# Two transformer layers with routed experts on one core: deeper row buffers and a pinned scaling in the last stage of layer 1

## The chip, the cores and the metric

The kernel runs on one core of a Trainium2 chip. The metric is the device time of one execution in microseconds (us), taken as the median of several runs. A core has five engines that work side by side, each through its own queue of instructions in order: TensorE (PE in the profile; its weight loads are PEld), VectorE (DVE), ScalarE (ACT), GpSimd (POOL) and SyncE (SP). [...] Transfers go out from the queues of SP (loads and stores) and of POOL (gathers by index) to 16 DMA engines that all of them share.

## The reference

The input is a residual stream x of 4 sequences of 512 rows with 512 features, 2048 rows in all. Each of the two layers computes

    xn = layernorm(x)
    x  = x + attention(xn) + experts(xn)

Layer 0 has a sparse and local attention with 16 heads of 128 and eight experts, of which each row takes two. Layer 1, where the change is, has a plain softmax attention with 16 heads of 32, and this feed-forward part:

    logits = xn @ router_w;  the best two of 8 experts, gates = softmax of the two
    combined = gate0 * silu(xn @ W[e0]) + gate1 * silu(xn @ W[e1])
    y = xn + combined @ proj_w + proj_b
    result = norm_w * y / sqrt(mean(y*y) + 1e-6)

Everything is float32. The last stage of the kernel, called the mixing here, is the lower three lines of this block, mixed with the last groups of layer 1's attention.

## The kernel before, in words

**Tiles.** The 2048 rows are 16 tiles of 128 rows (`n` = 0 to 15). The experts have written their results to a table `yd` in memory, one row for each pair of row and expert. The attention runs over 16 groups `g` (sequence `b`, four heads `j`), each with four steps `kc` of 128 keys: scores `st` (L1322), their exponentials `pT` on ACT (L1324), the context `cx` (L1336), and on DVE the running sum `pS` of the exponentials (L1342, two instructions a step from `kc` = 1 on). Beside them run the queries and keys of the next group (`qp`, L1298, finished on DVE in L1303 to L1313), once per group the sum over keys (`sm`, L1350) with reciprocals (L1360) and the scaled context (L1368), for the last sequence its values by seven products (`vp`, L1258, finished on DVE in L1262 to L1272), and for each tile of rows the attention's output product (`o`, L1405).

**Who sets the order.** A list `jobs1` puts each step of the experts and of the mixing at a place (g, kc). For tile n the mixing has four steps at four places one behind the other:

    for d, f in ((0, mix), (1, turn_mix), (2, project_mix), (3, finish_mix)):
        jobs1.append((at[here + d], lambda n=n, f=f: f(n)))

with `here` moving on by 13 places for 16 tiles. `mix` issues two gathers on POOL for the two expert rows of each token (`row0`, `row1`, L545), a load of xn (`xa`, L1435), the two gate scalings on DVE (L1438 and L1439), and adds the bias on POOL (L1440). `turn_mix` transposes the sum on PE (`trc`, L1447) and copies it out on ACT (`combT`, L1451). `project_mix` multiplies by proj_w on PE (`po`, L1458), adds the product to xa on DVE (L1459), squares on ACT (L1462) and forms the inverse root on POOL (`yss`, L1463 and L1464). `finish_mix` scales on DVE (L1469) and adds the result to the residual row.

**The order on an engine.** Within these places the order of instructions on each engine is chosen when the program is built, by the framework's scheduler; `tc.keep_in_program_order` keeps an instruction where the program has it. In `mix` the first scaling of tiles 0 and 1 is kept so (`pin`), that of the later tiles is not.

**Residual rows.** The two parts of a row's result, attention (`way` 0) and mixing (`way` 1), arrive at different times. `bring` (L1390) loads the old residual row from memory (`accd`) into a free place, `add_part` (L1394) adds a part on DVE and then stores the row, to `out` (L1397) where both parts are in, and back to `accd` (L1399) where one is still to come. If the row lies already in one place for the other part, nothing is loaded.

**Banks.** The products `vp`, `qp`, `trc`, `po`, `o` and `sm` take turns in three PSUM banks (`bank1("mm", ...)`). PE can begin the product after the next two only when the reader of the first, on DVE or ACT, is done. The DVE instructions that free a bank are L1264 to L1272, L1303 to L1313, L1394 (for `o`) and L1459; ACT frees those of `trc` and `sm`.

**Buffers.** In the mixing's pool each name has two buffers if nothing else is said. The gathered rows have one buffer each, so POOL gathers tile n+1's `row0` when PE has transposed tile n's, and its `row1` when DVE has used tile n's.

Of the kernel before, what the change touches and what calls it, by code (L numbers as in the profile page):

```python
# [12 lines left out]
F32 = mybir.dt.float32  # L13
I32 = mybir.dt.int32
AF = mybir.ActivationFunctionType
ALU = mybir.AluOpType
# [4 lines left out]
P = 128  # L21
B, S, HID = 4, 512, 512
# [3 lines left out]
KC = HID // P  # L26
# [23 lines left out]
def two_layers(ctx: ExitStack, tc: tile.TileContext, a: dict, out: bass.AP, large: bass.AP):  # L50
# [4 lines left out]
    V, G, A, PE = nc.vector, nc.gpsimd, nc.scalar, nc.tensor  # L55
# [20 lines left out]
    def load(pool, name, shape, src):  # L76
        t = pool.tile(shape, F32, tag=name, name=name, bufs=1)
        nc.sync.dma_start(out=t, in_=src)
        return t
# [376 lines left out]
    def at_rows(idx):  # L456
        return bass.IndirectOffsetOnAxis(ap=idx, axis=0)

    class Experts:
# [80 lines left out]
        def gather(self, n):  # L540

            rs = []
            for k in range(2):
                x = self.pool.tile([P, HID], F32, tag=f"row{k}", name=f"row{k}_{self.r.name}_{n}")
                G.indirect_dma_start(out=x, out_offset=None, in_=self.yd,  # L545
                                     in_offset=at_rows(self.r.slot[:, k, n : n + 1]))
                rs.append(x)
            return rs
# [87 lines left out]
    rout = {}  # L636
# [544 lines left out]
    rows = {"wv_b": load(w1p, "wv_b", [P, HID], a["wv_b"].partition_broadcast(P))}  # L1181
# [3 lines left out]
    NJ = NH1 * D1 // P  # L1185
# [88 lines left out]
    def queries(g, i):  # L1274
        b, j = groups1[g]
        if i == 0:
            qk[g] = ap_.tile([P, 2, S], F32, tag="qk", name=f"qk_{g}")
        if b:
            return queries7(g, i)
        qp_ = bank1("mm", f"qp_{g}_{i}")  # L1280
        for k in range(KC):
            PE.matmul(qp_, lhsT=wa[("wqT", "wkT")[i]][:, k, ts(j, P)], rhs=xnT[:, k, ts(b, S)],
                      start=(k == 0), stop=(k == KC - 1))
        V.tensor_scalar(qk[g][:, i, :], qp_, qkb[:, i, j : j + 1], None, ALU.add)
# [30 lines left out]
    def weights(g, kc):  # L1315

        pt = ap_.tile([P, HJ, S], F32, tag="pT", name=f"pT_{g}_{kc}")
        for pair in range(HJ // 2):
            st = psum1("st", f"st_{g}_{kc}_{pair}", 2)
            for i in range(2):  # L1320
                rows_ = ds((2 * pair + i) * D1, D1)
                tc.keep_in_program_order(PE.matmul(st[:, i, :], lhsT=qk[g][rows_, 1, ts(kc, P)], rhs=qk[g][rows_, 0, :],  # L1322
                                                   start=True, stop=True))
            A.activation(pt[:, ts(pair, 2), :], st, AF.Exp, scale=SCALE1)  # L1324
        return pt
# [3 lines left out]
    def attend(g, kc, pt):  # L1329
        b, j = groups1[g]  # L1330
        if kc == 0:
            acc_cx[g] = psum1("cx", f"cx1_{g}")[:, 0, :]
            acc_pt[g] = ap_.tile([P, HJ, S], F32, tag="pS", name=f"pS_{g}", bufs=1)
            first_pt[g] = pt
        for h in range(HJ):
            tc.keep_in_program_order(PE.matmul(acc_cx[g][ds(h * D1, D1), :], lhsT=v[b][:, kc, ds(j * P + h * D1, D1)], rhs=pt[:, h, :],  # L1336
                                               start=(kc == 0), stop=(kc == TC - 1)))

        if kc > 0:
            before = first_pt.pop(g) if kc == 1 else acc_pt[g]  # L1340
            for pair in range(HJ // 2):
                V.tensor_tensor(acc_pt[g][:, ts(pair, 2), :], before[:, ts(pair, 2), :], pt[:, ts(pair, 2), :], ALU.add)  # L1342
# [3 lines left out]
    def sum_keys(g):  # L1346

        sm = bank1("mm", f"sm1_{g}")
        for h in range(HJ):
            PE.matmul(sm[ds(h * D1, D1), :], lhsT=ones, rhs=acc_pt[g][:, h, :], start=True, stop=True)  # L1350
        del acc_pt[g]
        cs = ap_.tile([P, S], F32, tag="cs", name=f"cs_{g}", bufs=1)
        A.copy(cs, acc_cx.pop(g))
        rs = ap_.tile([P, S], F32, tag="rsum", name=f"rsum_{g}", bufs=1)
        A.activation(rs, sm, AF.Copy, accum_out=ends[:, 1, g : g + 1])
        parts[g] = cs, rs

    def invert(g, t):
        rs = parts[g][1]
        V.reciprocal(rs[:, ts(t, P)], rs[:, ts(t, P)])  # L1360
# [12 lines left out]
    def scale_context(g):  # L1373
        scale_chunk(g)
        largest_sum(g)
# [4 lines left out]
    def bring(n, way):  # L1380

        if (n, 1 - way) in lies:
            lies[n, way] = lies[n, 1 - way]
            return
        if n < NT - TC:

            lies[n, way] = acc[:, 3 * TC + n % TC, :] if way else xnT[:, 3 if n + 1 < NT - TC else 0, 0:S]
        elif left[n] == 2:
            lies[n, 0] = lies[n, 1] = acc[:, n, :]
        nc.sync.dma_start(out=lies[n, way], in_=accd[ts(n, P), :])  # L1390

    def add_part(n, part_, way):
        x = lies.pop((n, way))
        V.tensor_tensor(x, x, part_, ALU.add)  # L1394
        left[n] -= 1
        if left[n] == 0:
            nc.sync.dma_start(out=out_v[n], in_=x)  # L1397
        elif (n, 1 - way) not in lies:
            nc.sync.dma_start(out=accd[ts(n, P), :], in_=x)  # L1399

    def output1(b, t):
        n = b * TC + t
        op = bank1("mm", f"o1_{n}")
        for jj in range(NJ):
            PE.matmul(op, lhsT=cT1[b][:, jj, ts(t, P)], rhs=wa["woT"][:, jj, :],  # L1405
                      start=(jj == 0), stop=(jj == NJ - 1))
        add_part(n, op, 0)
# [23 lines left out]
    def mix(n):  # L1431

        g0, g1 = rout["ex1"].gather(n)
        x = rout["mix"].tile([P, HID], F32, tag="xr", name=f"xa_{n}")
        nc.sync.dma_start(out=x, in_=xnd[ts(n, P), :])  # L1435

        pin = tc.keep_in_program_order if n < 2 else (lambda x: x)
        pin(V.tensor_scalar(g0, g0, r1.gate[:, 0, n : n + 1], None, ALU.mult))  # L1438
        V.scalar_tensor_tensor(g0, g1, r1.gate[:, 1, n : n + 1], g0, ALU.mult, ALU.add)  # L1439
        G.tensor_tensor(x, x, rows["pb"], ALU.add)  # L1440
        held[n] = g0, x

    def turn_mix(n):
        g0, x = held[n]
        tr = bank1("mm", f"trc_{n}")
        for f in range(KC):
            PE.transpose(tr[:, ts(f, P)], g0[:, ts(f, P)], ident)  # L1447
        bring(n, 1)
        cT_ = rout["mix"].tile([P, KC, P], F32, tag="xT", name=f"combT_{n}")

        A.activation(cT_, tr.rearrange("p (k t) -> p k t", k=KC), AF.Copy, scale=0.5)  # L1451
        held[n] = cT_, x
# [13 lines left out]

    def finish_mix(n):
        y, ss = held.pop(n)
        V.scalar_tensor_tensor(y, y, ss[:, 0:1], rows["nw1"], ALU.mult, ALU.mult)  # L1469
        add_part(n, y, 1)  # L1470


# [30 lines left out]
    for n in range(NT):  # L1503
        here = first + n * 13 // 16
        for d, f in ((0, mix), (1, turn_mix), (2, project_mix), (3, finish_mix)):
            jobs1.append((at[here + d], lambda n=n, f=f: f(n)))
# [30 lines left out]
    for g in range(NG):  # L1537
        b, j = groups1[g]
        for kc in range(TC):
            nxt = weights(g, kc)  # L1540
            if late is not None:
                attend(*late)
            late = (g, kc, nxt)
            if g > 0:
                if kc == 1:
                    sum_keys(g - 1)
                    invert(g - 1, 0)
                if kc == 2:
                    invert(g - 1, 1)
                    invert(g - 1, 2)  # L1550
                if kc == 3:
                    invert(g - 1, 3)
                    scale_context(g - 1)
            if kc < 2 and g + 1 < NG:
                queries(g + 1, kc)
            if kc > 1 and j + 1 == NJ and 1 < b + 1 < B:
                values7(b + 1, kc - 2)

            if kc == 1 and g > NJ:
                bring(g - NJ - 1, 0)  # L1560
            if kc == 2 and g + 1 == NG:
                bring(NT - TC - 1, 0)
            if kc == 3 and g > NJ:
                output1(*divmod(g - NJ - 1, TC))
            run1((g, kc))
# [716 lines left out]
```

## Time and profile before

| | us |
|---|---|
| median of 3 runs | 2043.84 |
| lowest, highest | 2041.92, 2044.12 |
| the profiled execution | 2039.16 |
| its span, first to last instruction | 2037.1 |
| outside the span | 2.1 |
| PE busy in the span | 1983.6 (97%) |
| DVE busy | 1506.5 (74%) |
| ACT busy | 868.5 (43%) |
| POOL busy | 746.3 (37%) |
| mean granted TensorE clock | 0.995 |

The span is counted from the first instruction; all places in time below are us from there. The mixing begins at about 1845 us, when the last product of the experts is done, and its last scaling runs at about 2008 us. Behind it the last outputs of the attention end the span. Times of groups of instructions are given with their line, the engine, the operation and the tiles written and read. "[1.12 <-DVE xnT L1394]" behind a row of the timeline says that the engine stood idle for 1.12 us ahead of it, and that an L1394 instruction on DVE ended the wait.

### The profile page before, as it was taken

The page shows a single profiled execution, that of the slowest core. Times are in us where ns is not written, and L with a number is a line of the kernel's source. Part 1 is how long each engine was busy: PE and PEld are TensorE (multiplying, and loading weights), DVE is VectorE, ACT ScalarE, POOL GpSimd, SP SyncE. Part 2 cuts the span into 40 slices and gives each one's busy share as a digit, 9 for nine tenths or more (in the row PEclk, how much of TensorE's full clock was granted, in tenths as well). Part 3 has the DMA queues.
Part 4 walks back from the last instruction along what each step waited for, and adds up shares of the span by engine and source line. Part 5 has one row for each costly group of instructions (what it writes and reads, how often), then busy time and mean ns, then how long its engine had stood idle before and what let it go on. Part 6 is the DMA issues. An engine that isn't in the chain of part 4 may idle for free.

```text
span 2037.1 us, 28573 instructions
## 1 busy us (share of the span) xinstructions
PE 1983.6 (97%) x9358; PEld 1243.6 (61%) x9358; DVE 1506.5 (74%) x3696; ACT 868.5 (43%) x2600; POOL 746.3 (37%) x761
## 2 busy tenths in 40 slices
PE   7999999999999999999999999999999999999998
PEld 4666667777777777767667666666334445445443
DVE  7889968777776777786678878788596555557775
ACT  4554444444444444444444454454244432332332
POOL 4423144443323333344343444353114332322550
PEclk8999999999999999999999999999999999999999
DMA  7101133333433343245443222121317775773551
GB/s 254 69 33 62 43 120 123 145 109 114 126 133 104 115 153 104 96 135 186 183 161 118 73 89 74 42 74 64 121 55 253 271 255 194 270 245 112 154 161 59
DMA packets 98909, 267.27 MB, mean 131 GB/s; under 512 B 14400, under 2 KB 27840, under 8 KB 87488
## 3 DMA queue, kind: packets, MB, share of 16 engines
q0 software_dynamic: 27072, 148.91, 21.6%
q1 hardware_dynamic: 70528, 114.34, 16.7%
q10 hardware_dynamic: 1152, 2.10, 0.3%
q8 instruction: 77, 1.26, 0.3%
q14 instruction: 80, 0.66, 0.1%
HBM read 222.05 MB, written 42.73 MB: 130 GB/s over the span
## 4 chain that ended last, share of the span: by engine, by line
PE 81%; DVE 9%; ACT 3%; POOL 2%; issue 2%; DMA 1%; ACTq 0%; DVEq 0%; SPq 0%; POOLq 0%
PE p L675 25%; PE hp_r L529 12%; PE op L842 4%; PE st L767 4%; PE sp L758 2%; PE st L1322 2%; PE ox L873 2%; PE qp L1298 2%; PE cx L1336 2%; PE ca L811 2%; DVE pS L1342 2%; PE o L1405 2%; PE oz L873 2%; PE trm_r L517 1%; PE trq L695 1%
## 5 line engine op out<-in xcount | busy, mean ns | idle before, releaser
L529 PE MATMUL hp_r<-we_r,xT_r 128*128 128x512 f32 (+1 forms) x592 | 224.7, 596 | 2.7 <-ACT xT_r L519 2.2
L481 POOL DMA_INDIRECT xr_r<-xnd,rows_r x72 | 87.5, 1216 | 342.2 <-PE trm_r L517 299.0
L775 POOL TENSOR_TENSOR lT<-lT,lmask 128x512 f32<-128x512 f32 (+1 forms) x128 | 152.6, 1200 | 129.1 <-ACT lT L771 128.9
L675 PE MATMUL p<-wT,x 128*128 128x384 f32 x512 | 178.7, 492 | 0.8 <-DVE wT L119 0.8
L675 PE MATMUL p<-wB,x 128*128 128x384 f32 x512 | 176.2, 488 | 3.0 <-DVE u L731 3.0
L675 PE MATMUL p<-wA,xnT 128*128 128x384 f32 x512 | 174.3, 492 | 0.3 <-DVE u L710 0.2
L575 ACT ACTIVATE sq<-qb 128x128 f32<-128x128 f32 x384 | 118.9, 310 | 96.2 <-DVE qb L724 45.8
L1324 ACT ACTIVATE pT<-st 128x1024 f32<-128x1024 f32 x128 | 123.3, 1014 | 62.5 <-PE st L1322 56.7
L529 PEld LDWEIGHTS hp_r<-we_r,xT_r 128*128 128x128 f32 (+1 forms) x592 | 83.0, 170 | 98.8 <-issue 92.5
L675 PEld LDWEIGHTS p<-wB,x 128*128 128x128 f32 x512 | 93.7, 190 | 67.1 <-issue 9.6
L675 PEld LDWEIGHTS p<-wA,xnT 128*128 128x128 f32 x512 | 95.5, 193 | 61.6 <-issue 3.3
L675 PEld LDWEIGHTS p<-wT,x 128*128 128x128 f32 x512 | 94.2, 192 | 62.7 <-issue 5.5
L689 ACT ACTIVATE qb<-qb,ss 128x128 f32<-128x128 f32 x256 | 81.9, 390 | 106.6 <-POOL ss L578 104.5
L519 ACT COPY xT_r<-trm_r 128x512 f32<-128x512 f32 x72 | 41.9, 581 | 193.4 <-PE hp_r L529 180.8
L767 PE MATMUL st<-qkT 128*128 128x256 f32 (+1 forms) x512 | 114.7, 354 | 1.5 <-ACT qkT L702 1.5
L771 ACT ACTIVATE lT<-st,ss 128x256 f32<-128x256 f32 (+1 forms) x128 | 49.0, 446 | 153.0 <-PE st L767 153.0
L545 POOL DMA_INDIRECT row_r<-yd,slot_r x64 | 75.0, 1172 | 89.8 <-DVE row_r L1439 37.6
L767 PEld LDWEIGHTS st<-qkT 128*128 128x128 f32 x512 | 92.2, 190 | 11.9 <-ACT qkT L702 1.7
L578 POOL TENSOR_TENSOR ss<-ss,nhalf 128x6 f32<-128x6 f32 x64 | 95.4, 1490 | 5.3
L842 PE MATMUL op<-Wo,cT 128*128 128x512 f32 x208 | 93.7, 595 | 0.4 <-DVE lv L739 0.4
L577 POOL TENSOR_SCALAR ss<-ss 128x6 f32<-128x6 f32 x64 | 31.0, 485 | 164.3 <-ACT sq L575 163.9
L675 PE MATMUL p<-wT,xnT 128*128 128x384 f32 x256 | 88.0, 486 | 0.0
(384 smaller groups left out, 4632.7 us busy)
## 6 DMA issues: line engine op xcount, KB each, us to landing
x<-xsd SPq DMA_DIRECT2D x112, 256.0 KB, 3.2
yd<-yr_r SPq DMA_DIRECT2D x72, 256.0 KB, 4.4
wA<-in_wA SPq DMA_DIRECT2D x16, 384.0 KB, 3.9
wB<-in_wB SPq DMA_DIRECT2D x16, 384.0 KB, 7.6
xnd<-xn SPq DMA_DIRECT2D x24, 256.0 KB, 2.1
accd<-acc SPq DMA_DIRECT2D x18, 256.0 KB, 2.0
acc<-in_x SPq DMA_DIRECT2D x16, 256.0 KB, 4.9
Wo<-in_Wo SPq DMA_DIRECT2D x8, 512.0 KB, 3.7
```

Source lines behind the costliest of these rows:

```text
L481: G.indirect_dma_start(out=out, out_offset=None, in_=src, in_offset=at_rows(idx))
L529: PE.matmul(hp[ts(h, m), :], lhsT=xT[:, k, ts(h, m)], rhs=w[:, ts(k, HID)], start=(k == 0), stop=(k == KC - 1))
L545: G.indirect_dma_start(out=x, out_offset=None, in_=self.yd, in_offset=at_rows(self.r.slot[:, k, n : n + 1]))
L575: A.activation(sq, x[:, h, :], AF.Square, accum_out=ss[:, h : h + 1])
L578: pin(G.tensor_tensor(ss, ss, nhalf[:, 0:n], ALU.pow))
L675: PE.matmul(p, lhsT=x[:, k, ts(c, P)], rhs=w[:, k, :], start=(k == 0), stop=(k == 1))
L689: A.activation(x[:, j, :], x[:, j, :], AF.Copy, scale=sq[t][:, j : j + 1])
L767: PE.matmul(st[:, ds((t % 2) * 256, n)], lhsT=qkT[:, HG + h, ts(t, P)], rhs=qkT[:, h, ds(t * P, n)], start=True, stop=True)
L775: G.tensor_tensor(dst, dst, lmask.rearrange("p a w j -> p (a w j)")[:, 0:n], ALU.mult)
L842: PE.matmul(op, lhsT=cT[:, h, ts(t, P)], rhs=wo[:, h, :], start=(h == 0), stop=(h == HG - 1))
L873: PE.matmul(p[:, ts(c, 256)], lhsT=left[:, ts(c, P)], rhs=right, start=new and c == 0, stop=True, skip_group_check=True)
L1324: A.activation(pt[:, ts(pair, 2), :], st, AF.Exp, scale=SCALE1)
```

## The change

The change has five parts. In layer 1 (`self.silu`) the gathered rows get three buffers each instead of one. The xn rows (`xa`) get four buffers instead of two, the transposed sums (`combT`) three instead of two. The scaling in `finish_mix` is kept in program order. And `bring` for the attention's part of tile g-5 is called in step `kc` = 0 of group g instead of step 1.

```diff
@@ gather, L541 @@
             for k in range(2):
-                x = self.pool.tile([P, HID], F32, tag=f"row{k}", name=f"row{k}_{self.r.name}_{n}")
+                x = self.pool.tile([P, HID], F32, tag=f"row{k}", name=f"row{k}_{self.r.name}_{n}",
+                                   bufs=3 if self.silu else 1)
                 G.indirect_dma_start(out=x, out_offset=None, in_=self.yd,
                                      in_offset=at_rows(self.r.slot[:, k, n : n + 1]))
                 rs.append(x)
@@ mix, L1431 @@
         g0, g1 = rout["ex1"].gather(n)
-        x = rout["mix"].tile([P, HID], F32, tag="xr", name=f"xa_{n}")
+        x = rout["mix"].tile([P, HID], F32, tag="xr", name=f"xa_{n}", bufs=4)
         nc.sync.dma_start(out=x, in_=xnd[ts(n, P), :])
@@ turn_mix, L1446 @@
         bring(n, 1)
-        cT_ = rout["mix"].tile([P, KC, P], F32, tag="xT", name=f"combT_{n}")
+        cT_ = rout["mix"].tile([P, KC, P], F32, tag="xT", name=f"combT_{n}", bufs=3)
@@ finish_mix, L1467 @@
         y, ss = held.pop(n)
-        V.scalar_tensor_tensor(y, y, ss[:, 0:1], rows["nw1"], ALU.mult, ALU.mult)
+        tc.keep_in_program_order(V.scalar_tensor_tensor(y, y, ss[:, 0:1], rows["nw1"], ALU.mult, ALU.mult))
         add_part(n, y, 1)
@@ loop over groups and steps, L1556 @@
-            if kc == 1 and g > NJ:
+            if kc == 0 and g > NJ:
                 bring(g - NJ - 1, 0)
```

Since tile 9's row still lies in place for the other part when it is asked for a step sooner, one load from `accd` and one store to it are no longer issued. A kept instruction also moves its neighbours: in the changed program the last scalings of tiles 0, 1, 5, 6, 10 and 11 stand behind the attention's `o` additions of tiles 7, 8 and 9, where they stood ahead of them. PE's order is the same in both programs.

## The prediction

> **What bounds the kernel.** I read the totals and the slices first: PE is busy for 97% of the span, so only PE's idle and slow stretches can be won. Then PE's waits in the stretch that the change touches, 1845 to 2016 us:
>
> ```profile
> PE 1983.6 (97%) x9358; PEld 1243.6 (61%) x9358; DVE 1506.5 (74%) x3696; ACT 868.5 (43%) x2600; POOL 746.3 (37%) x761
> ...
> PE qp L1298 <- DVE xnT L1394: 3.1, 2, 2.0
> PE po L1458 <- DVE acc L1394: 2.2, 1, 2.2
> PE trc L1447 <- DVE qk L1311: 1.3, 2, 1.0
> PE po L1458 <- DVE xa L1459: 0.9, 2, 0.5
> PE sm L1350 <- DVE pS L1342: 0.7, 1, 0.7
> ```
>
> These are totals, number and longest. All of them end on DVE instructions that free one of the three PSUM banks. They make about 9 us. The timeline of PE shows what follows the two longest:
>
> ```profile
> 1895.74 1.99 PE L1298 MATMUL qp<-xnT,wqT 128*128 128x256 f32 x8 [1.12 <-DVE xnT L1394]
> ...
> 1939.11 3.68 PE L1298 MATMUL qp<-xnT,wqT 128*128 128x256 f32 x8 [2.01 <-DVE xnT L1394]
> ...
> 1982.81 5.37 PE L1458 MATMUL po<-pw,combT 128*128 128x512 f32 x8 [2.15 <-DVE acc L1394]
> ```
>
> Eight `qp` take 1.99 us after a wait of 1.12, but 3.68 after one of 2.01; eight `po` take 5.37 after 2.15, against 3.60 elsewhere. So a wait of 2 us costs another 1.69 to 1.77 at a lower clock (the granted clock is 0.96 in 1914 to 1960 and in 1960 to 2004, and 1.00 before). Then DVE's and POOL's waits, which tell why DVE is late:
>
> ```profile
> DVE xa L1469 <- POOL yss L1464: 28.7, 14, 3.5
> DVE row_r L1438 <- DMA row_r<-yd,slot_r: 4.5, 6, 1.7
> ...
> POOL row_r L545 <- DVE row_r L1439: 37.6, 11, 10.5
> ```
>
> DVE stands 28.7 us before the last scaling, with bank-freeing additions queued behind it. POOL stands 37.6 us before gathers whose only buffer is in use. The ceiling of the change is therefore 9.2 us of waits and 3.5 of slow clock, 12.7 us or 0.6%. About 0.2% (4.1 us) is what a measurement of this kernel can tell from no change.
>
> **The change, part by part.** All sums are against the profiled execution (2039.16, of which 2037.1 are span); it lies 4.7 under the median, and I carry differences over to the median of 2043.84.
>
> *Kept scaling.* In the new order L1469 and its L1394 of tiles 0 and 1 stand behind the L1394 of o_7, those of 5 and 6 behind o_8, of 10 and 11 behind o_9. No instruction is added. The wait for yss no longer holds up o's addition, but the L1459 of the next tile now stands behind two such pairs. From the rows, a pair moves DVE on by 1.40 (L1469 at 1889.27, its L1394 at 1890.06, the next at 1890.67), two by 2.8. L1459 of tile 2 frees the bank for qp67_14, which PE wants 1.84 after qp12_14.
>
> *Three row buffers.* Gathers run ahead, and POOL's 37.6 us shrink, hidden anyway. But POOL's queue is in order too: in the new order `row1_7` (waiting for DVE's L1439 of tile 4) and yss_0 stand ahead of `row0_5`, and DVE's L1438 of tile 5 ahead of two pS and o_7's addition. Walked with the old durations: L1439 of tile 4 ends at 1883.8, gather row1_7 to 1885.1, yss_0 to 1886.0, gather row0_5 issued 1886.2; in quiet stretches a gather lands 3.3 to 4.2 after issue, so L1438 can start at 1889.5 to 1890.4. With 0.4, 1.13, 0.7, 1.13 and 0.6 for what follows, o_7's addition ends at 1893.7 to 1894.5. PE wants it at 1894.6: the 1.12 wait goes. L1459 of tile 2 then ends at 1897.1 to 1897.9, but PE wants it at 1896.5: a new wait of 0.6 to 1.4. Won there: 0.
>
> The same walk for the other waits: at 1913.78, L1438 of tile 7 can start at about 1907 instead of 1909.40, so the 1.02 go. At 1926.76 and 1930.92, L1459 of tiles 5 and 6 no longer wait for yss: 0.7 won. At 1939.11, `row0_10` is held behind row1_12 and yss_5 and lands at about 1931, o_8's addition ends around 1935.4 and PE, by then 2 us ahead of the old times, wants it at 1935.1: 0.3 wait, then 1.6 for L1459 of tile 7. Of 2.01 is won 0.1, and of the slow 1.69 half, as 1.6 lies between the 1.12 that kept the clock and the 2.01 that did not: 1.0 together. At 1970.31 and 1974.49: 0.7. At 1982.81 no row1 gather stands ahead of row0_15 and no qp follows; 0.3 of 2.15 stays, with the slow 1.77 gone: 3.6. Before the last `sm` the two pS no longer wait behind tile 15's scaling: 0.7. Sum: 0 + 1.0 + 0.7 + 1.0 + 0.7 + 3.6 + 0.7 = 7.7 us won.
>
> *What the buffers bring forward.* Scalings of tiles from 2 on are not kept in place. With free buffers, tile 2's L1438 now stands on DVE between L1264 and L1265, and its L1439 between L1265 and L1266, still in the middle of the values. This is the old timeline there:
>
> ```profile
> 1848.09 0.69 DVE L1264 TENSOR_TENSOR xnT<-vp,xnT 128x512 f32<-128x512 f32 x1 [0.43 <-PE vp L1258]
> 1849.81 0.69 DVE L1265 TENSOR_TENSOR xnT<-vp,xnT 128x512 f32<-128x512 f32 x1 [1.03 <-PE vp L1258]
> ...
> 1849.88 0.95 POOL L545 DMA_INDIRECT row_r<-yd,slot_r  x1 [0.30 <-issue]
> ...
> 1855.33 1.89 PE L1258 MATMUL vp<-acc,xnT 128*128 128x256 f32 x8
> 1857.06 3.60 PE L1405 MATMUL o<-woT,cT 128*128 128x512 f32 x8
> ```
>
> Tile 2's gathers are POOL's fifth and sixth: after 1849.88 with a pitch of 1.25 they go out at 1851.1 and 1852.4. They cannot land soon. The first four landed 9.0, 8.2, 8.0 and 7.5 after issue, at 1854.6, 1855.6, 1856.6 and 1857.4, since pw (1 MB), pb, nw and two xa come in at the same time:
>
> ```profile
> pw<-in_pw SPq DMA_DIRECT2D x1, 1024.0 KB, 5.9
> xa<-xnd SPq DMA_DIRECT2D x2, 256.0 KB, 8.8
> ...
> row_r<-yd,slot_r POOLq DMA_INDIRECT x4, 8.1
> ```
>
> With the old landing pitch of about 1 us the fifth and sixth land at 1858.4 and 1859.4. The two more xa loads, which four buffers let SP issue right behind the first two, make 1 MB more in all; at the 353 to 417 GB/s of 1852 to 1856 that is 2.7 us, so 1860.1. I take 1859.7 for the sixth. DVE then needs 0.75 (L1439), 0.6 (L1266), 2.3 (two pS) and 0.68 (L1268): 1864.0. o_6 needs the bank that L1268 frees and began at 1857.06: PE is 6.9 us late there. It has also stood about 4 us before vp p3 (L1265 can end only at 1859.5), so a slow stretch follows; vp p3 takes most of it inside the wait, and I charge half of 1.77: 0.9. Loss 7.8 us.
>
> Here two rules of the Trainium skill bear on the sum. The row first: 7.5 to 9.0 us to landing in this burst, 3.3 to 4.2 outside it. "DMA: Bandwidth & Descriptors" ("Anatomy of one DMA — SWDGE (gpsimd) path") gives about 2.0 us plus bytes over 436 GB/s, an estimate of 2.6 us for 256 KB: the sixth gather would be there at 1855.0, DVE through at 1859.3, and the loss 2.2 to 3. The same page ("Queues, rings and completion order") says that each DMA engine takes turns between the queues that have work, which speaks against the change: more transfers make all later. The burst's own rows decide, so 7.8. Second, "TensorE: Matmul & The Clock Gate" (Part 1) puts the fall to half rate behind an idle window of about 3.4 us. By it the 2.01 and 2.15 waits would have kept the clock, and 2.6 of my 7.7 would not be there to win; the trace has them slow, and the measurement counts.
>
> *Earlier bring, combT, xa later on.* bring's loads land in 2 to 3 us and are wanted two places later; one load and one store of 256 KB fall away on SP. No PE or DVE wait before L1394 ends on a load in the trace, so 0; without that cover a late row would cost at most its landing, 2.6. SP's accd store of o_6 now stands behind the two xa issues (0.6 each), also 0. combT's third buffer: no wait of PE ends on a missing combT buffer, 0.
>
> Net: 7.8 − 7.7 = +0.1.
>
> **Rivals.**
> *The start is cheap (faster).* If the fifth and sixth gathers land 3.8 us after issue, at 1856.2, L1268 ends at 1860.5 and PE loses 3.4 plus some clock, 4; if the wait before qp67_15 stays short enough for the full clock, 9 are won. Net −5, 2039. For it: the queues are filled before these two go out. Against: the fourth gather took 7.5, and these stand behind it in the same queue.
> *The middle of the stage gets worse (slower).* The gathers for tiles 5 and 10 stand on DVE ahead of o's addition. If they land 1.2 us later than walked, the first place has waits of about 0.8 and 1.9, with 1.7 of slow clock, against 1.12 before (3.3 lost), the second 1.5, 2.0 and 1.7 against 3.7 (1.5 lost), the third still wins 2.5, and 3.1 come from the small ones: 0.8 won in place of 7.7. With the start's 7.8 that is +7, 2051. It decides from about 0.9 us of lateness on. For it: a gather beside a busy DVE took up to 2.14 us on POOL instead of 0.95 (at 1922.46). Against: three buffers leave the row1 halves landed long before.
> *The change does not do what it says*: the order is fixed in the program, so only the lead of the gathers can fail, and that is the case above.
>
> **How the numbers follow.** Both large terms are of equal size. Balanced within 4.1 us: 0.43, alone 2040.5 to 2047.5. Cheap start: 0.22. Worse middle or a start of 9 to 10 us: 0.35, weighted above the cheap start because every unknown of this program is a landing time, and landings in bursts come late. The time is 2044.0 (2043.84 + 0.1). The range takes in most of both other cases: 2036 to 2052.
>
> **What would show it.** In the new trace DVE should stand idle before L1438 from 1849 to about 1858.5, PE before vp p3 about 4 us and o_6 start near 1864; then no wait on L1394 over 1 us, DVE's wait on yss far below 28.7, a new PE wait on L1459 before qp, and `po` after o_9 at full clock. I am wrong if o_6 starts before 1861, or if qp still waits 2 us in both cycles.

## The result and the profile after

| | before | after |
|---|---|---|
| median of 6 runs, us | 2043.98 | 2052.81 |
| lowest, highest, us | 2041.72, 2044.88 | 2049.93, 2055.86 |
| ratio of the times, 95% interval | 1 | 1.0043 [1.0034, 1.0053] |

The change costs 8.8 us, 0.43%. The forecast of no measurable change is wrong. The profiled execution of the changed kernel is its slowest one, 2055.86 us (span 2054.1, mean granted clock 0.992), 16.7 over the profiled execution of before. Of these 16.7 us, 4.5 lie ahead of the mixing, where both programs do the same: the first gather is issued at 1850.13 instead of 1845.58. So I compare the two traces from the first gather on, and lay a time of the new trace back by 4.54 where I call it "in old time". All lines from L545 of the old kernel on have moved by one: the row scalings are now L1439 and L1440, the bias addition L1441, `trc` L1448, `po` L1459, its addition L1460, the last scaling L1470, the addition of a part L1395, `o` L1406.

Two points of the description ahead of the prediction have to be set right first. The gathered rows had two buffers each before the change, not one: their tiles come from the mixing's pool, which gives every name two if nothing else is said. The old trace shows it, as four gathers go out from 1845.58 to 1849.88, long before the first scaling at 1867.21; in the run e3 below, where one buffer is asked for, only two do. So the change takes the rows from two buffers to three, and in the old kernel it was tile n+2's `row0` that was gathered when PE had transposed tile n's. No term of the prediction's sum rests on the wrong count, but e3, e10 and e11 read differently with the right one. And no load or store has gone: both traces have 27 loads by `bring` and 11 stores back to `accd` by `add_part`, and only the place of one row has moved. The prediction had put that at 0.

The stage, from the first gather to the block of 24 products at the end of the attention (L1576), took 170.78 us before and takes 183.28 now. Cut at the same instructions:

| stretch, us | before | after | difference |
|---|---|---|---|
| first gather to the end of o_6 | 15.00 | 25.03 | +10.0 |
| to po_3 | 38.72 | 38.43 | −0.3 |
| to po_8 | 45.05 | 46.51 | +1.5 |
| to trc_14 | 43.67 | 45.29 | +1.6 |
| to the 24 products | 28.34 | 28.02 | −0.3 |

The first row is the start of the stage, the four others (+2.5) its middle and end. PE's busy time does not show which product had to wait, so next come PE's waits in 1840 to 2035 us of the new trace (engine, instruction, who ended the wait: us in total, times, longest):

```profile
PE trc L1448 <- DVE qk L1312: 6.0, 3, 3.4
PE vp L1259 <- DVE xnT L1266: 4.7, 1, 4.7
PE qp L1299 <- DVE xnT L1395: 1.8, 1, 1.8
PE o L1406 <- DVE v L1269: 1.5, 1, 1.5
PE o L1406 <- DVE xa L1460: 1.0, 1, 1.0
...
PE po L1459 <- DVE xnT L1395: 0.2, 1, 0.2
```

The wait of `vp` and that of `o` on L1269 are new and belong to the start. `trc` waited 1.3 in all and now waits 6.0. `qp` keeps one wait of 1.8. What the change was to remove is gone in full in one place only: `po` behind o_9 waits 0.2 instead of 2.2. DVE's waits in the same stretch:

```profile
DVE row_r L1439 <- DMA row_r<-yd,slot_r: 33.2, 8, 5.8
DVE row_r L1439 <- DMA xa<-xnd: 10.3, 1, 10.3
...
DVE xa L1470 <- POOL yss L1465: 3.3, 3, 1.8
```

The wait for yss has fallen from 28.7 us to 3.3, as the kept scaling should do. In its place DVE stands in front of the first scaling, for data on its way: 4.5 us before, 33.2 and 10.3 now. The start in the timeline, DVE first, then PE (start, duration, engine, line, operation, in brackets the idle time ahead and its releaser):

```profile
1852.62 0.69 DVE L1265 TENSOR_TENSOR xnT<-vp,xnT 128x512 f32<-128x512 f32 x1 [0.43 <-PE vp L1259]
1863.59 0.49 DVE L1439 TENSOR_SCALAR row_r<-row_r,gate_r 128x512 f32<-128x512 f32 x1 [10.27 <-DMA xa<-xnd]
1863.99 0.69 DVE L1266 TENSOR_TENSOR xnT<-vp,xnT 128x512 f32<-128x512 f32 x1
...
1865.90 3.43 DVE L1343 TENSOR_TENSOR pS<-pS,pT 128x1024 f32<-128x1024 f32 x2
1869.25 0.68 DVE L1269 TENSOR_TENSOR v<-xnT,vp 128x512 f32<-128x512 f32 x1
```

```profile
1864.73 3.78 PE L1259 MATMUL vp<-acc,xnT 128*128 128x256 f32 x8 [4.70 <-DVE xnT L1266]
1869.98 5.25 PE L1406 MATMUL o<-woT,cT 128*128 128x512 f32 x8 [1.47 <-DVE v L1269]
1875.16 1.14 PE L1323 MATMUL st<-qk 32*128 32x512 f32 x8
```

Tile 2's first scaling stands between L1265 and L1266 and holds DVE for 10.27 us. The profile names a load of `xa` that arrived last, which L1439 does not read; the semaphore that it waits for is that of the gather issued at 1855.68, whose last part arrives at 1863.56, and the run with two xa buffers below (e4) names the gather too. The banks stay occupied behind it, PE stands before `vp` and before `o`, and both run slowly: eight `vp` take 3.78 instead of 1.89, eight `o` 5.25 instead of 3.60. The granted clock is 0.50 from 1862.89 to 1873.13 and 1.00 before and after. Then the middle, three places on PE:

```profile
1929.15 1.09 PE L1448 MATMUL trc<-ident,row_r 128*128 128x128 f32 x8 [2.38 <-DVE qk L1312]
...
1954.73 3.50 PE L1299 MATMUL qp<-xnT,wqT 128*128 128x256 f32 x8 [1.84 <-DVE xnT L1395]
...
1976.65 1.97 PE L1448 MATMUL trc<-ident,row_r 128*128 128x128 f32 x8 [3.38 <-DVE qk L1312]
1978.55 2.09 PE L1323 MATMUL st<-qk 32*128 32x512 f32 x8
1980.57 1.93 PE L1337 MATMUL cx<-pT,v 128*32 128x512 f32 x8
```

The releaser L1312 is only the last link. This is the chain ahead of the first of the three, on POOL and DVE:

```profile
1915.81 1.38 POOL L1441 TENSOR_TENSOR xa<-xa,pb 128x512 f32<-128x512 f32 x1 [2.37 <-DMA xa<-xnd]
...
1917.78 1.03 POOL L546 DMA_INDIRECT row_r<-yd,slot_r  x1 [0.58 <-DVE xnT L1307]
...
1918.98 1.28 POOL L1441 TENSOR_TENSOR xa<-xa,pb 128x512 f32<-128x512 f32 x1 [0.18 <-DMA xa<-xnd]
...
1920.41 0.97 POOL L546 DMA_INDIRECT row_r<-yd,slot_r  x1 [0.15 <-issue]
...
1924.36 0.90 DVE L1439 TENSOR_SCALAR row_r<-row_r,gate_r 128x512 f32<-128x512 f32 x1 [5.12 <-DMA row_r<-yd,slot_r]
```

The gather at 1920.41 is `row0_7`. Its buffer came free when PE had transposed tile 4, by 1917.6. It left 2.8 us later, as POOL's queue had tile 4's bias addition, a gather of tile 9 and tile 5's bias addition ahead of it, and the first of these waited 2.37 for its xa row. It landed 3.95 after issue. DVE waits for it 5.12 and then has L1440, a pS, a reciprocal and two more instructions to do before L1312 frees the bank. Tile 12 repeats this five tiles later: `row0_12` leaves at 1967.03, 2.9 after PE has transposed tile 9, and DVE waits 5.81 for it until 1971.78.

### The profile page after: what moved, and what is told of

The parts are those of the page before. It is cut to its first block, busy times and chain, and to the rows that moved or that the text cites. A ratio compares the mean times of both kernels' runs of the same rounds, so it can differ in the third digit from the quotient of the medians.

```text
span 2054.1 us, 28543 instructions
## 1 busy us (share of the span) xinstructions
PE 1989.3 (97%) x9358; PEld 1245.4 (61%) x9358; DVE 1509.8 (74%) x3696; ACT 869.7 (42%) x2600; POOL 745.0 (36%) x761
## 4 chain that ended last, share of the span: by engine, by line
PE 77%; DVE 9%; POOL 3%; issue 3%; ACT 3%; DMA 2%; DVEq 0%; ACTq 0%; POOLq 0%
PE p L676 24%; PE hp_r L529 12%; PE op L843 4%; PE st L768 4%; PE sp L759 2%; PE ox L874 2%; PE st L1323 2%; DMA row_r<-yd,slot_r 2%; PE ca L812 2%; PE cx L1337 2%; DVE pS L1343 2%; PE oz L874 2%; PE qp L1299 1%; PE trq L696 1%; PE trm_r L517 1%
```

## Experiments

In the recorded expectations START names the theory that the loss is the start's, caused by tile 2's scaling amid the values. MIDDLE says that the rest of the stage has become worse too. Of the middle, PLACE says that the cause is where DVE's order puts the first scalings. POOL says that `row0_7` leaves late because of the additions ahead of it, LANDING that it lands late whenever it leaves. Ratios are to the kernel before, run on the same chip. A kernel made from the changed one is told from it by its diff, one made from the kernel before says so. All stretches of time count from the first gather. A table of all runs stands at the end of this section. Where an expectation speaks of one row buffer in the kernel before, read two.

**e1: the first scaling of tile 2 is kept in its place too.**

```diff
-        pin = tc.keep_in_program_order if n < 2 else (lambda x: x)
+        pin = tc.keep_in_program_order if n < 3 else (lambda x: x)
```

> The changed kernel, with the first scaling of tile 2 kept in program order as well (n < 3 instead of n < 2), so that it no longer stands on DVE in the middle of the values. Theory START: the wait of DVE before tile 2's scaling costs PE 10.0 us (14.58 of shift at the st behind o_6, less the 4.54 by which the whole stage began later in that execution), and all else nets to nothing or a little won; then o_6 starts within 1 us of its old distance from the stage's first gather (11.5 us), and the time is 2041 to 2044. Theory MIDDLE: PE meets the same late gathers for tiles 5, 7, 10 and 12 whenever it arrives, and PE's waits there (2.4 and 3.4 before trc, 1.8 before qp) are the cause; then they are still there, or greater, and the time stays at 2047 or more.

2042.66 us, ratio 1.0000 [0.9991, 1.0008]. The start takes 14.99 us, as before the change, so its 10 us are due to the place of this one instruction, and buffers, loads and gathers cost the start nothing by themselves. The stage takes 170.55 against 170.78: the middle, freed from the start, wins nothing. START gave the time, MIDDLE's waits are there all the same, in the places of the changed kernel:

```profile
1916.02 1.09 PE L1448 MATMUL trc<-ident,row_r 128*128 128x128 f32 x8 [2.45 <-DVE qk L1312]
...
1941.02 1.99 PE L1299 MATMUL qp<-xnT,wqT 128*128 128x256 f32 x8 [1.79 <-DVE xnT L1395]
1944.39 1.13 PE L1299 MATMUL qp<-acc 128*128 128x256 f32 x4 [1.38 <-DVE xa L1460]
1961.94 1.37 PE L1448 MATMUL trc<-ident,row_r 128*128 128x128 f32 x8 [2.54 <-DVE qk L1312]
```

**e2: the kept last scaling alone,** in the kernel before.

```diff
-        V.scalar_tensor_tensor(y, y, ss[:, 0:1], rows["nw1"], ALU.mult, ALU.mult)
+        tc.keep_in_program_order(V.scalar_tensor_tensor(y, y, ss[:, 0:1], rows["nw1"], ALU.mult, ALU.mult))
```

> The kernel before with the last scaling kept in program order, and nothing else of the change. Theory START: nothing stands before the values, the additions of o_7, o_8 and o_9 no longer wait for yss, and some of the 9.2 us of waits and 3.5 us of slow clock go: 2037 to 2041. Theory MIDDLE: behind the kept scaling DVE waits for gathers instead, as each row has one buffer; waits before qp stay and the time is 2042 to 2046.

2052.61 us, ratio 1.0050 [1.0037, 1.0064]. Both theories missed: no start loss, and 10 us lost all the same. DVE's wait tells how:

```profile
DVE xa L1460 <- POOL xa L1441: 15.5, 3, 6.0
```

With two xa buffers, a last scaling that stands behind o's addition holds its buffer longer. The next xa row is loaded later, POOL adds the bias later, and DVE's L1460 waits for that; `po` then waits 3.92 and 4.93 on PE. So the kept scaling does not pay alone; e9 shows that with the first scalings kept too it pays even with two xa buffers.

**e3: the changed kernel with one row buffer.**

```diff
-                                   bufs=3 if self.silu else 1)
+                                   bufs=1)
```

> The changed kernel with one buffer for each gathered row instead of three; xa, combT, the kept scaling and the earlier bring stay. Theory START: tile 2's scaling goes back behind tile 1's, the start is as before, so the time is 2037 to 2042 and close to the run with the kept scaling alone. Theory MIDDLE: without the lead of the gathers the waits of DVE for landings grow, and the time is over 2044.

2065.77 us, ratio 1.0110 [1.0095, 1.0125]. START missed, MIDDLE's side was right. On PE:

```profile
PE trc L1448 <- DVE row_r L1440: 26.1, 5, 9.5
```

This is not the row buffering of the kernel before but one buffer less: the third gather leaves only at 1871.90, when tile 0 has been scaled. One buffer brings the gathers too late for the transposition itself (e2, with two, has no such wait on PE). So the run prices one buffer against three, and does not say whether the kept scaling needs the third; e11 bears on that.

**e4: the row buffers alone,** in the kernel before.

```diff
-                x = self.pool.tile([P, HID], F32, tag=f"row{k}", name=f"row{k}_{self.r.name}_{n}")
+                x = self.pool.tile([P, HID], F32, tag=f"row{k}", name=f"row{k}_{self.r.name}_{n}",
+                                   bufs=3 if self.silu else 1)
```

> The kernel before with three buffers for each gathered row, and nothing else of the change. Theory START: the wait at the start is there with its full price, 10 us, and nothing is won in the middle since the last scaling still waits for yss ahead of o's addition: 2051 to 2056, with vp p3 waiting 4 to 5 us. Theory MIDDLE: the gathers' lead takes away DVE's waits for landings ahead of the additions, and only half of the start is left at the end: 2046 to 2049.

2052.45 us, ratio 1.0051 [1.0038, 1.0065]. The time is that of START, its split is not: the start costs 7.6 us instead of 10 (22.64 against 15.00), and the rest of the stage another 3.1 (181.53 in all). The start loss comes with the row buffers alone, and DVE's longest wait is put down to the gather:

```profile
1863.13 3.46 PE L1259 MATMUL vp<-acc,xnT 128*128 128x256 f32 x8 [3.90 <-DVE xnT L1266]
1868.33 3.70 PE L1406 MATMUL o<-woT,cT 128*128 128x512 f32 x8 [1.74 <-DVE v L1269]
```

```profile
DVE row_r L1439 <- DMA row_r<-yd,slot_r: 12.5, 5, 9.5
```

o_6 starts 19.01 us after the first gather, against 11.48 before and 19.85 in the changed kernel. The two xa rows more that SP loads in the burst therefore cost about 0.8 us, if nothing else in the start differs; that was not tried by itself. The other 1.6 between 7.6 and 10.0 are the clock: here `o` runs at 3.70, as the clock is at half from 1862.71 to 1866.12 only.

**e5: e1 with six xa buffers,** paid for with a combT and a ysq buffer, so that POOL's additions need not wait for their rows.

```diff
-        x = rout["mix"].tile([P, HID], F32, tag="xr", name=f"xa_{n}", bufs=4)
+        x = rout["mix"].tile([P, HID], F32, tag="xr", name=f"xa_{n}", bufs=6)
-        pin = tc.keep_in_program_order if n < 2 else (lambda x: x)
+        pin = tc.keep_in_program_order if n < 3 else (lambda x: x)
-        cT_ = rout["mix"].tile([P, KC, P], F32, tag="xT", name=f"combT_{n}", bufs=3)
+        cT_ = rout["mix"].tile([P, KC, P], F32, tag="xT", name=f"combT_{n}", bufs=2)
-        sq = rout["mix"].tile([P, HID], F32, tag="th", name=f"ysq_{n}")
+        sq = rout["mix"].tile([P, HID], F32, tag="th", name=f"ysq_{n}", bufs=1)
```

> The changed kernel with tile 2's scaling kept as in the run before, and six xa buffers instead of four (combT two, the squares one, for space). DVE's and PE's order stay the same as with tile 2's scaling kept; on POOL only the bias additions of xa move two tiles forward. Theory POOL QUEUE: the row0 gathers of tiles 7 and 12 are late because POOL's queue holds them behind bias additions whose xa loads are late (POOL waits 14.0 us for xa in the run with tile 2 kept); with six buffers they leave 2.5 to 3 us sooner, PE's waits of 2.45 and 2.54 before trc fall under 0.5, and the time is 2036 to 2039. Theory LANDING: the gathers are late because they are asked for only when PE has transposed tile n-3, and take 4 us to land; the waits before trc stay over 1.5 and the time is 2041 to 2044.

2040.98 us, ratio 0.9988 [0.9982, 0.9995]. This run does not decide between POOL and LANDING. The scheduler moved POOL's additions two tiles ahead, and the one that now stands ahead of `row0_7` is that of xa_6, which waits for tile 0's buffer to be free. The gather still leaves 3.1 us after tile 4's transposition, and `trc` still waits 2.90 and 2.60. What is gone is most of the wait of `qp` on L1395 (1.79 to 0.27).

**e6: every first scaling is kept in its place.**

```diff
-        pin = tc.keep_in_program_order if n < 2 else (lambda x: x)
+        pin = tc.keep_in_program_order if True else (lambda x: x)
```

> The changed kernel with the first scaling of every tile kept in program order, not only of tiles 0 and 1. Each scaling then stands about two tiles later on DVE than in the changed kernel, and gathers have 10 us or more to land. Theory PLACE: what costs is where the scheduler puts the scaling of gathered rows, ahead of additions that free banks; DVE's wait for landings (31 us with tile 2 kept) falls under 8, o's additions come 4 us sooner, and of PE's waits before qp (1.79, 1.38) and trc (2.45, 2.54) nothing over 1 is left: 2031 to 2037, faster than both kernels. Theory LATE SCALING: kept so late, the scaling is what PE's transposes wait for (trc <- DVE row_r, up to 9.5 us with one row buffer), and the time is 2042 or more.

2024.56 us (4 runs, 2024.35 to 2027.15), ratio 0.9908 [0.9892, 0.9923], 18.8 us under the kernel before: the best version of all, better than I expected. PE's waits in 1840 to 2045 are one line, and the values on DVE run as they did before the change:

```profile
PE trc L1448 <- DVE qk L1312: 0.2, 1, 0.2
```

```profile
1851.52 0.69 DVE L1265 TENSOR_TENSOR xnT<-vp,xnT 128x512 f32<-128x512 f32 x1 [0.43 <-PE vp L1259]
1853.25 0.69 DVE L1266 TENSOR_TENSOR xnT<-vp,xnT 128x512 f32<-128x512 f32 x1 [1.03 <-PE vp L1259]
```

Its busy times by windows (PE, PEld, DVE, ACT, POOL with numbers of instructions, then granted clock, share of the DMA engines, GB/s):

```profile
1864.00:1902.00 38.00, 37.76 (x183) 18.97 (x183) 26.81 (x40) 16.18 (x26) 16.23 (x17) 1.00 0.39 122
1902.00:1940.00 38.00, 38.00 (x167) 18.24 (x166) 32.43 (x45) 14.71 (x27) 24.77 (x25) 1.00 0.52 161
1940.00:1979.00 39.00, 39.00 (x163) 17.34 (x162) 34.83 (x46) 14.54 (x26) 21.31 (x24) 1.00 0.56 177
```

PE works without a gap at full clock from 1902 to 1979. DVE has no wait on a gather left among its longest ones. The stage takes 154.95 us, 15.8 less than before, and 28.3 less than in the changed kernel: 10.0 at the start and 18.3 behind it. The program issues the same work, only DVE's order differs and with it what the scheduler makes of the rest. That settles PLACE against LATE SCALING. The 3 us by which the medians differ more than the stages lie outside the stage and are not explained.

**e7: e6 with the buffers of e5** (six xa, two combT, one ysq).

> The run with every first scaling kept, and six xa buffers besides. Theory POOL QUEUE and PLACE together: if no gather is urgent any more, the order of POOL does not matter, and this is within 1.5 us of the run with four xa buffers. If late xa loads delay L1459 itself, it is 2 to 4 us faster than that run.

2025.37 us, ratio 0.9911 [0.9898, 0.9925], the same as e6, as expected. With every scaling in its place, more xa buffers have nothing left to win.

**e8: row buffers and every first scaling kept, the last scaling free,** in the kernel before.

```diff
+                                   bufs=3 if self.silu else 1)
...
-        pin = tc.keep_in_program_order if n < 2 else (lambda x: x)
+        pin = tc.keep_in_program_order if True else (lambda x: x)
```

> The kernel before with three row buffers and every first scaling kept, but the last scaling free, two xa buffers and the bring where it was. Theory PLACE: the start is as before, DVE's waits for landings are gone, but the last scaling still waits for yss ahead of the additions of o_7, o_8 and o_9, so the waits of 1.12, 2.01 and 2.15 stay: 2039 to 2043. If it is as fast as the run with the last scaling kept (2031 to 2037), then the last scaling's place was never the cost.

2041.16 us, ratio 0.9988 [0.9982, 0.9995], as expected. DVE's wait for yss is the old one (28.3 us), and PE's costliest wait is again that before `po`:

```profile
1978.20 5.37 PE L1459 MATMUL po<-pw,combT 128*128 128x512 f32 x8 [2.31 <-DVE xa L1460]
```

So the kept last scaling is needed for e6's gain, though alone it lost 10 us. Its own share shows in e9, which differs from this run in nothing else: 0.9945 against 0.9988.

**e9: e6 without the other parts of the change** (two xa and two combT buffers, `bring` in step 1).

```diff
-        x = rout["mix"].tile([P, HID], F32, tag="xr", name=f"xa_{n}", bufs=4)
+        x = rout["mix"].tile([P, HID], F32, tag="xr", name=f"xa_{n}")
-        pin = tc.keep_in_program_order if n < 2 else (lambda x: x)
+        pin = tc.keep_in_program_order if True else (lambda x: x)
-        cT_ = rout["mix"].tile([P, KC, P], F32, tag="xT", name=f"combT_{n}", bufs=3)
+        cT_ = rout["mix"].tile([P, KC, P], F32, tag="xT", name=f"combT_{n}")
-            if kc == 0 and g > NJ:
+            if kc == 1 and g > NJ:
```

> Of the change only the three row buffers and the kept last scaling, with the first scaling of every tile kept as well; xa has two buffers, combT two, and the bring is in step 1 as before. Theory PLACE: the two kept scalings and the row buffers carry the gain, and this is within 2 us of the run with all of the change and every first scaling kept (2024.6). Theory XA: the late last scaling holds the two xa buffers too long, as in the run with the kept scaling alone (DVE waited 15.5 us for POOL's bias addition there), PE waits 4 to 5 us before po two or three times, and the time is 2034 to 2042.

2030.84 us, ratio 0.9945 [0.9928, 0.9962]: faster than before, and by the ratios 0.37% (7.5 us) short of e6. That is worse than PLACE allowed and better than XA. The place of the trouble is that of e2:

```profile
DVE xa L1460 <- POOL xa L1441: 10.6, 5, 3.1
```

The other parts are worth something once the scalings stand right, the xa buffers most likely. They were not split further.

**e10 and e11: e6 with one and with two row buffers.**

```diff
-                                   bufs=3 if self.silu else 1)
+                                   bufs=1)
```

```diff
-                                   bufs=3 if self.silu else 1)
+                                   bufs=2 if self.silu else 1)
```

> The run with all of the change and every first scaling kept, but with one buffer for each gathered row. The gather of tile n then leaves only when PE has transposed tile n-1, and the scaling kept in its place waits for it. Theory PLACE: the row buffers are what lets the scaling be late without a wait; here trc waits for the scaling by 5 to 9 us in each of three cycles, 2055 to 2068. If the time stays under 2035, the place of the scaling alone did it.

> The same with two buffers for each gathered row. Theory PLACE: a gather has from the transposes of tile n-2 to the scaling of tile n, about one place of 10 us where tiles are one place apart, but about 1 us less than landing takes where two tiles share a place (tiles 1, 6 and 11): 2025 to 2034, between one buffer and three.

One buffer: 2064.29 us, ratio 1.0108 [1.0091, 1.0125]. Two: 2033.03, 0.9946 [0.9929, 0.9963]. Three (e6): 0.9908. Both times lie where they were expected. On PE, first of e10, then of e11:

```profile
PE trc L1448 <- DVE row_r L1440: 26.5, 5, 9.5
```

```profile
1929.90 3.70 PE L1406 MATMUL o<-woT,cT 128*128 128x512 f32 x8 [1.44 <-DVE xa L1460]
...
1971.59 5.40 PE L1406 MATMUL o<-woT,cT 128*128 128x512 f32 x8 [2.14 <-DVE xa L1460]
```

One buffer, fewer than the kernel before has, is too few with the scalings in either order (e3). With that kernel's two, the kept scalings and the other parts of the change already win 0.54%, more than half of e6's gain; the third buffer is worth the other 0.38%. What cost the time in the changed kernel is the freedom that the third buffer gives the scheduler.

All runs, with what distinguishes them (combT's third buffer and the earlier bring go with the runs that have four or six xa buffers, except that e5 and e7 have two combT buffers):

| run | row buffers | xa | last scaling kept | first scaling kept | ratio |
|---|---|---|---|---|---|
| before | 2 | 2 | no | tiles 0, 1 | 1 |
| e2 | 2 | 2 | yes | tiles 0, 1 | 1.0050 |
| e4 | 3 | 2 | no | tiles 0, 1 | 1.0051 |
| e8 | 3 | 2 | no | all | 0.9988 |
| e9 | 3 | 2 | yes | all | 0.9945 |
| after | 3 | 4 | yes | tiles 0, 1 | 1.0043 |
| e1 | 3 | 4 | yes | tiles 0 to 2 | 1.0000 |
| e5 | 3 | 6 | yes | tiles 0 to 2 | 0.9988 |
| e6 | 3 | 4 | yes | all | 0.9908 |
| e7 | 3 | 6 | yes | all | 0.9911 |
| e11 | 2 | 4 | yes | all | 0.9946 |
| e10 | 1 | 4 | yes | all | 1.0108 |
| e3 | 1 | 4 | yes | tiles 0, 1 | 1.0110 |

Not run: the kernel before with every first scaling kept and nothing else.

## Why the prediction was wrong

**The start: mechanism right, size too small.** Tile 2's scaling stood where the order of instructions put it, and DVE waited for it. In old time the fifth gather landed at 1859.0 and the sixth at 1860.0, against 1858.4 and 1859.7 in the walk. Of the two prices set beside each other, the burst's own rows were right; by the estimate of 2.6 us from the Trainium skill's figures ("DMA: Bandwidth & Descriptors", "Anatomy of one DMA — SWDGE (gpsimd) path") the sixth would have been there at 1855.0. Two terms behind the landing were mis-sized. The two pS took 3.43 instead of 2.3, while POOL was at a gather and bias additions, as in e4 (3.42, beside a gather and one addition); whether POOL's work slows them was not tried. And the slow clock cost o_6 1.65 where I charged 0.9, half of it. The charge came from the slow stretches behind the 2 us waits; here the clock had fallen to half at 1862.89, in the wait before `vp`, and stayed there for 10.24 us, to 1873.13, well into `o`. So o_6 starts 8.4 later instead of 6.9, and the start costs 10.0 instead of 7.8. e1, without the wait, and e4, with the row buffers alone, confirm the cause from both sides.

**The middle: the step that failed.** I had 7.7 us won; in the profile 2.5 are lost. The forecast gain behind o_9 came (`po` waits 0.24 instead of 2.15, at 3.67 instead of 5.37), the small waits on yss at 1970.31 and 1974.49 went, and so did the wait before `sm`. The failed step is the walk of the row0 gathers to the waits of `trc`: "L1438 of tile 7 can start at about 1907 instead of 1909.40, so the 1.02 go", and nothing at all for tile 12. In the run that scaling starts at 1910.4, laid back by the 14.0 us that PE is late in the product ahead, and `trc` waits 2.38. I had let `row0_7` leave as soon as its buffer was free. POOL held it for 2.8 us behind bias additions whose own rows were late. The trace of before already had this in the same place, for the gather that waits for the same transposition (done by 1903.6; the scaling behind it, at 1909.40, is tile 6's there):

```profile
1904.44 1.28 POOL L1440 TENSOR_TENSOR xa<-xa,pb 128x512 f32<-128x512 f32 x1 [0.63 <-DMA xa<-xnd]
...
1905.87 0.97 POOL L545 DMA_INDIRECT row_r<-yd,slot_r  x1 [0.16 <-issue]
```

It landed 3.4 us after issue, at 1909.3 and not at 1907. The 3.3 to 4.2 us to landing were too narrow as well: outside the burst the 27 gathers of the old trace's mixing that can be timed took 3.3 to 5.3 us, in the median 4.1, and `row0_12` took 4.75. I had named POOL's order for tiles 5 and 10, but not walked it for 7 and 12. At tile 12 there was no wait before and I walked none; it has become the longest one of the middle, 3.38 with 2.7 us of slow clock (1.97, 2.09 and 1.93 for what takes 1.09, 1.14 and 1.06 at full clock). Of the 10.2 us between 7.7 won and 2.5 lost, 6.1 lie at tile 12 and 2.4 at tile 7. Another 1.3 lie at 1926.76 and 1930.92, where PE waits 1.02 and 0.32 for L1460 instead of 0.25 and 0.47, and 0.9 at 1939.11, where `qp` waits 1.84 and then runs slowly at 3.50. Tile 10's gather went out behind yss_5 and a row1 gather, as walked, but only at 1946.90, and DVE could start with it at 1950.66, with the additions of `o` behind it. Against these, 0.5 were won at 1895.74, where I had none.

**The rivals.** The worse middle (2051 us) has the time almost right and the mechanism half right: late gathers ahead of bank-freeing work on DVE, but worst at tiles 7 and 12 before `trc`, while the place at tile 5 that it named shows only 0.64 before `qp`. That its time is so near is in part luck, as its start was 2.2 too cheap. The cheap start is refuted.

**The ceiling was too low.** I put it at 9.2 us of waits and 3.5 of slow clock. (The five lines shown make 8.2 of the 9.2; the rest are 0.5 before `o` on L1459 and 0.5 before `cx`, which ends on ACT and frees no bank.) e6 shortened the stage by 15.8: the four later stretches took 154.95 − 15.00 = 139.95 us, 15.8 less than in the kernel before, of which the last stretch alone gave 3.4. There products had run longer than they do in e6 (`st` 1.66 instead of 1.14, `cx` 1.97 instead of 1.10, `sm` 2.19 instead of 1.70, 1.9 us in all), and these I had not counted. About 1.2 us remain unexplained.

**Medians and profiles.** In the stage the two profiles differ by 12.5, the medians by 8.8 us. The profiled execution of after is 3.05 over its median, so that the profile's middle (+2.5) shows an execution with more losses there than most. With the start at its 10.0 from e1, the medians leave a middle of about −1. e1 has an even middle too (170.55 against 170.78), with its waits of 2.45 and 2.54 before `trc` and hardly any slow clock. So the middle is about even by the medians and 2.5 lost in the profile, and in neither reading are 7.7 us won.

**What stays open.** Whether the late leave of `row0_7` on POOL alone makes the wait of `trc`, or its 4 us of landing would do so by itself, e5 did not tell. My estimate, from the 2.8 and 2.9 us that POOL held the gathers, is that leaving at once would have taken all of the 2.38 and most of the 3.38; no run shows it. That the wait matters only because DVE's order puts the scaling ahead of L1312 is shown by e6.

## What to carry to other kernels

More buffers let a scheduler hoist a consumer as well as its load. Fix the consumer's place at the same time, or it waits at the head of an in-order queue, in front of work that frees banks for the engine that bounds the kernel. Here the third row buffers alone cost 0.5%, the kept last scaling alone 0.5%, the whole change with the scheduler free on the first scalings 0.4%, and with those kept in place as well it won 0.9%. Before you count buffers, look up what the pool gives by itself, and check it by the number of loads that go out at once. When a change's walk lets a gather leave "as soon as its buffer is free", go through every instruction ahead of it on the issuing queue, for each tile of the cycle.

## What the runs showed of the hardware that was not expected

The clock's fall does not follow the length of the last wait. After waits of 1.84 (after, `qp`), 2.14 (e11, `o`) and 2.31 us (e8, `po`) the next eight products ran at 3.50, 5.40 and 5.37 instead of 1.99, 3.60 and 3.60. After 2.38 (after, `trc`) and 2.45 us (e1, `trc`) they took 1.09, and after 1.79 (e1, `qp`) 1.99, the full rate.

The record of the granted clock shows what it does follow. In each trace its changes in the mixing lie on a grid of 3.41 us, and the stretches at half clock last 3.41, 6.83 or 10.24 us. These are such windows of the changed kernel (from and to, length, PE's busy time with the number of products, granted clock, share of the DMA engines, GB/s), first around the wait of 1.84 before `qp`, then around that of 2.38 before `trc`:

```profile
1951.64:1955.05 3.41, 1.57 (x14) 1.00 0.00 0
1955.05:1958.46 3.41, 3.41 (x9) 0.50 0.79 178
1924.34:1927.75 3.41, 2.43 (x6) 1.00 0.17 64
1927.75:1931.16 3.41, 2.01 (x16) 1.00 0.25 77
1931.16:1934.57 3.41, 3.09 (x17) 1.00 0.44 114
```

The shorter wait lies within one window and leaves PE 1.57 us of work in it; the next window is at half clock. The longer one is shared by two windows, with 2.43 and 2.01 us of work, and the clock stays. The count over all 13 traces of this case, from about 35 us on in each, says the same: after each of the 34 full-clock windows in which PE was busy for 46% or less the clock was at half; after the 7,556 with 47% or more it stayed full, but for one (58%, e8 at 2003.07, not explained). So whether a wait of about 2 us costs another 1.7 depends on where it falls in the grid, and the prediction's charges by the length of a wait could come out right only by chance. The Trainium skill ("TensorE: Matmul & The Clock Gate", Part 1) puts the fall behind an idle window of about 3.4 us; the length agrees with the grid, but a window need not be idle for it: here PE was busy in it for up to 46%.
